# A routed expert layer: from one region per expert to one region per pair of experts

## The chip, the cores and the metric

The kernel runs on one core of a Trainium2 chip. The metric is device time in microseconds of that core. The kernel before took 7589.02 us (median of three runs, 7568.02 to 7589.64). A separate execution, recorded by the hardware profiler, took 6768.39 us; its span from the first to the last instruction is 6766.6 us.

## The reference, cut to what matters

12,500 nodes with 256 features go through four layers, each added to its input: a relational graph convolution, a feed-forward layer on half of the nodes, a graph attention layer, and a mixture of experts. The change touches the mixture, and the end of the attention layer, where its routing is done.

```python
def _L1_ffn_ref(x, Wg, bg, W1, b1, W2, b2):
    B, S, D, E, H, K = (4, 512, 256, 8, 512, 2)
    gate_scores = x @ Wg + bg
    _, idx = jax.lax.top_k(gate_scores, K)
    mask = jax.nn.one_hot(idx, E, dtype=x.dtype).sum(axis=-2)
    xf = x.reshape(-1, Dv)
    mf = mask.reshape(-1, E)
    h = jax.nn.gelu(jnp.einsum('td,edh->teh', xf, W1) + b1[None], approximate=False)
    y = jnp.einsum('teh,ehd->ted', h, W2) + b2[None]
    out = jnp.einsum('ted,te->td', y, mf)
...
x = x + _L1_ffn_ref(_layernorm(x, axis=-1)[None], ...)[0]
```

So every token is multiplied with the weights of exactly two of eight experts, and the two results, their two biases b2 and the token itself are added up without a weight.

## The kernel before, in words

The edges are handled in 1661 tiles of 128. The relational layer and the attention layer each fetch one row per edge by an indirect gather on POOL (`gather`, L234), one instruction per tile, and sum them into nodes with matmuls against a one-hot matrix (L921). In the attention layer (`even_gat`) the order of all work is written out by a small planner: a step is one tile, and each piece of work is put at a step and may yield some steps between its parts. The engines' queues are then held to that order (`tc.manual_schedule`).

When the nodes of two windows of the attention layer are complete, a "quad" of four tiles of 128 nodes goes to `route` (L673). It normalizes the nodes, computes the eight gate scores, and makes a mask `mk` with a one at the two best experts (L697 to L713). Two small matmuls count, for each expert, how many tokens came before (L717, L718); `run` holds the totals. From these each token gets two slot numbers `toI`, one in each of its experts' regions of the DRAM table XS (L720 to L732). Then POOL scatters the normalized row, with its node number as a 257th element, twice: one indirect DMA per tile of 128 tokens and expert choice, eight per quad (L740). They are issued behind the latest gather (`behind`). Last, `route` multiplies the mask with the biases b2, adds the token itself and writes that to the DRAM table O2 (L747 to L760).

`finish` fills the ends of the eight regions with 256 empty slots each by 16 scatters (L774), and works out, for 105 groups of 256 slots, where each begins and which expert it has (`ATD`).

`slots` (L818) is the expert stage. It loads all weights into SBUF (Wall, 8 MB) and runs 105 groups. For each, SP reads the group's row and expert into registers (L848, L850), loads 256 slots (`xs`) and copies one expert's weights from Wall into `we` by a 1 MB DMA. PE transposes the slots, multiplies with W1 (L872), ACT applies gelu (L874), PE multiplies with W2 (L878), DVE copies the result out (L881), and POOL adds it to the rows of O2 by an indirect DMA that accumulates (L882), two per group. Since two experts add to the same row, these scatters are kept in order. At the end O2 is copied to `out` (L886, L889).

Of the kernel before, what the change touches and what calls it, by code (L numbers as in the profile page):

```python
# [30 lines left out]
SP = mybir.EngineType.SP  # L31
ORDERED = {mybir.EngineType.PE, DVE, mybir.EngineType.Activation, SP}
# [68 lines left out]
def gnn_ffn_kernel(ctx: ExitStack, tc: tile.TileContext, x, src, dst, etype, eweight, w_rel, wr, br,  # L101
# [542 lines left out]
    SLOTS = 256  # L644
    REGION = NM * P + SLOTS
    NG = (2 * N + NE * (SLOTS - 1)) // SLOTS
    KE = EH // P
    XS = dram.tile([(NE + 1) * REGION, D + 1], F32, name="XS")
    O2 = dram.tile([N + SLOTS, D], F32, name="O2")
    ATD = dram.tile([2, NG], I32, name="ATD")  # L650

    def router(st):
# [5 lines left out]
        b2s = wp.tile([NE, D], F32, name="b2s")  # L658
        nc.sync.dma_start(b2s, b2)
# [4 lines left out]
        region = wp.tile([P, NE], F32, name="region")  # L664
        nc.gpsimd.iota(region, pattern=[[REGION, NE]], base=0, channel_multiplier=0,
                       allow_small_or_imprecise_dtypes=True)
        run = wp.tile([P, NE], F32, name="run")
        nc.vector.tensor_copy(run, region)
        real = wp.tile([P, 1], F32, name="real")
        nc.vector.tensor_scalar(real, node[:, NM - 1:NM], float(N), None, op0=OP.is_lt)  # L670
        filled = []

        def route(ms, xg, wk, pst, psy, psc, behind=None):  # L673
# [4 lines left out]
            ln_stats(xg, mv[:, :G], wk)  # L678
            yield 3
            xe = wk.tile([P, 4, D + 1], F32, name="xe", bufs=3)  # L680
            nc.vector.tensor_copy(xe[:, :G, D], node[:, ms[0]:ms[0] + G])
            gt = wk.tile([P, 4, NE], F32, name="gt")
            pg = psc[0].tile([P, 4, NE], F32, name=psc[1])
            for i, m in enumerate(ms):
                normalized(xe[:, i, :D], xg[:, i, :], mv[:, i, :])
                yield 1
                pt = pst[0].tile([P, 2, P], F32, name=pst[1])
                for k in range(2):
                    transpose(pt[:, k, :], xe[:, i, k * P:(k + 1) * P])
                yield 1  # L690
                xT = wk.tile([P, 2, P], F32, name="xT")
                evac(xT, pt)
                yield 1
                for k in range(2):
                    nc.tensor.matmul(pg[:, i, :], xT[:, k, :], Wgs[:, k, :], start=k == 0, stop=k == 1)
# [18 lines left out]
            yield 1  # L714

            pp_ = psc[0].tile([P, 2, 4, NE], F32, name=psc[1])
            nc.tensor.matmul(pp_[:, 0, :G, :], before, mk[:, :G, :], start=True, stop=True)  # L717
            nc.tensor.matmul(pp_[:, 1, :G, :], ones, mk[:, :G, :], start=True, stop=True)  # L718
            yield 2
            pos = wk.tile([P, 4, NE], F32, name="pos")  # L720
            for i in range(G):
                nc.vector.tensor_tensor(pos[:, i, :], pp_[:, 0, i, :], run, op=OP.add)
                nc.vector.tensor_tensor(run, pp_[:, 1, i, :], run, op=OP.add)
            yield 1
            far = wk.tile([P, 4, NE], F32, name="far")
            nc.vector.tensor_scalar(far[:, :G, :], mk[:, :G, :], -float(NOWHERE), float(NOWHERE),
                                    op0=OP.mult, op1=OP.add)
            nc.vector.tensor_tensor(far[:, :G, :], far[:, :G, :], pos[:, :G, :], op=OP.add)
            nc.vector.tensor_tensor(pos[:, :G, :], pos[:, :G, :], mk[:, :G, :], op=OP.mult)
            toI = wk.tile([P, 2, 4], I32, name="toI", bufs=3)  # L730
            nc.vector.tensor_reduce(toI[:, 0, :G], far[:, :G, :], axis=AX.X, op=OP.min)
            nc.vector.tensor_reduce(toI[:, 1, :G], pos[:, :G, :], axis=AX.X, op=OP.max)  # L732
            yield 3
            for i, m in enumerate(ms):
                n = rows(m)
                for j in range(2):
                    if i or j:
                        yield 2
                    with tc.issue_after(behind().ins) if behind else nullcontext():
                        ins = nc.gpsimd.indirect_dma_start(  # L740
                            out=XS, out_offset=bass.IndirectOffsetOnAxis(ap=toI[:n, j, i:i + 1], axis=0),
                            in_=xe[:n, i, :], in_offset=None)
                    tc.declare_no_dep(ins.ins, group="slots", reason="each slot is written once")
                    tc.add_to_no_dep_group("slots", ins.ins)
                    filled.append(ins.ins.name)

            o = wk.tile([P, 4, D], F32, name="o")  # L747
            for i, m in enumerate(ms):
                pt = pst[0].tile([P, 2, P], F32, name=pst[1])
                transpose(pt[:NE, 0, :], mk[:, i, :])  # L750
                yield 1
                mT = wk.tile([NE, P], F32, name="mT")
                nc.scalar.activation(mT, pt[:NE, 0, :], AF.Copy)
                yield 1
                pb = psy[0].tile([P, D], F32, name=psy[1])
                nc.tensor.matmul(pb, mT, b2s, start=True, stop=True)
                yield 2
                nc.vector.tensor_tensor(o[:, i, :], pb, xg[:, i, :], op=OP.add)
                n = rows(m)
                nc.sync.dma_start(O2[m * P:m * P + n, :], o[:n, i, :])  # L760

        def finish():

            pad = wp.tile([P, SLOTS // P, D + 1], F32, name="pad")
# [931 lines left out]
```

## Time and profile before

| what | us |
|---|---|
| median of three runs | 7589.02 |
| profiled execution | 6768.39 |
| its span | 6766.6 |
| relational layer and feed-forward, gathers at full rate | about 500 to 2650 |
| attention layer with route | about 3000 to 5400 |
| end of route, padding, loading of the weights | 5400 to 5511 |
| expert stage, to the last scatter's landing | 5511 to 6723 |
| copy of O2 to out | 6723 to 6766.6 |

Over the whole span PE is busy 84%, DVE 43%, ACT 11%, POOL 57%. A busy share says little by itself: PE's clock is granted by a throttle, 0.734 of full speed on average here, and a slow PE looks busy. In a table of stretches each row has the stretch, its length, then busy time and number of instructions of PE, PE's weight loads, DVE, ACT and POOL, the granted clock, the busy share of the DMA engines and GB/s. In a list of groups a row has line, engine, operation, output<-input, shape and count, then busy time and mean ns of one, then the idle time before them and what ended it. "issue" is time in which the engine waited for nothing that the profile shows.

### The profile page before, as it was taken

The page shows a single profiled execution, that of the slowest core. Times are in us where ns is not written, and L with a number is a line of the kernel's source. Part 1 is how long each engine was busy: PE and PEld are TensorE (multiplying, and loading weights), DVE is VectorE, ACT ScalarE, POOL GpSimd, SP SyncE. Part 2 cuts the span into 40 slices and gives each one's busy share as a digit, 9 for nine tenths or more (in the row PEclk, how much of TensorE's full clock was granted, in tenths as well). Part 3 has the DMA queues.
Part 4 walks back from the last instruction along what each step waited for, and adds up shares of the span by engine and source line. Part 5 has one row for each costly group of instructions (what it writes and reads, how often), then busy time and mean ns, then how long its engine had stood idle before and what let it go on. Part 6 is the DMA issues. An engine that isn't in the chain of part 4 may idle for free. (4 is left out here: it accounts for less than half of the span.)

```text
span 6766.6 us, 77763 instructions
## 1 busy us (share of the span) xinstructions
PE 5684.5 (84%) x28042; PEld 4806.8 (71%) x28042; DVE 2938.0 (43%) x7741; ACT 753.3 (11%) x1553; POOL 3886.8 (57%) x3768
## 2 busy tenths in 40 slices
PE   6979999999999998548898899898998947777775
PEld 3447777777777786438888888888887836656664
DVE  6642333333333332766666666666666621111110
ACT  2320000000000001110000000000000011212121
POOL 0017777777777774047777777777777522222222
PEclk9986778777778878775555555555565668888887
DMA  7763333333333332455555555555555345555555
GB/s 244 303 259 107 114 113 109 112 111 114 113 112 114 113 113 75 149 157 139 141 142 142 142 140 145 141 142 142 143 141 138 105 148 140 140 140 133 136 145 153
DMA packets 437378, 949.51 MB, mean 140 GB/s; under 512 B 84371, under 2 KB 293222, under 8 KB 410783
## 3 DMA queue, kind: packets, MB, share of 16 engines
q0 software_dynamic: 199872, 494.39, 28.1%
q1 hardware_dynamic: 237108, 450.03, 21.3%
q8 instruction: 224, 3.67, 0.2%
q14 instruction: 174, 1.42, 0.1%
HBM read 617.71 MB, written 228.88 MB: 125 GB/s over the span
## 5 line engine op out<-in xcount | busy, mean ns | idle before, releaser
L234 POOL DMA_INDIRECT row<-T,rowC x1661 | 1668.3, 1004 | 567.1 <-issue 221.3
L234 POOL DMA_INDIRECT rows<-T1A,srcC x1661 | 1666.1, 1003 | 512.0 <-issue 428.1
L921 PE MATMUL bin<-S,rows 128*128 128x96 f32 (+5 forms) x8756 | 1822.6, 380 | 3.6 <-DVE rows L1269 3.3
L921 PEld LDWEIGHTS bin<-S,rows 128*128 128x128 f32 x8756 | 1739.3, 298 | 79.4 <-issue 67.7
L921 PEld LDWEIGHTS bin<-S,row 128*128 128x128 f32 x7700 | 1281.7, 247 | 333.8 <-DMA row<-T,rowC 206.2
L921 PE MATMUL bin<-S,row 128*128 128x96 f32 (+5 forms) x7700 | 1374.3, 335 | 118.7 <-DMA row<-T,rowC 105.2
L882 POOL DMA_INDIRECT O<-y,toI x210 | 326.9, 1556 | 911.1 <-DVE y L881 420.1
L872 PE MATMUL ph<-xT,we 128*128 128x256 f32 x1680 | 475.3, 446 | 270.7 <-DVE xT L191 265.7
L872 PEld LDWEIGHTS ph<-xT,we 128*128 128x128 f32 x1680 | 376.0, 229 | 349.2 <-DVE xT L191 278.8
L930 DVE TENSOR_TENSOR S<-lcC,col 128x576 f32<-128x576 f32 x554 | 415.4, 750 | 395.5 <-PE bin L921 395.2
L1269 DVE TENSOR_TENSOR rows<-rows,pw 128x1536 f32<-128x1536 f32 x277 | 482.9, 1743 | 30.9 <-PE pw L195 30.8
L861 DVE CAST toI<-xs 128x2 int32<-128x2 f32 x105 | 17.7, 169 | 1024.0 <-DMA O<-y,toI 812.7
L1001 PE MATMUL ph<-xT,w1s 128*128 128x512 f32 (+1 forms) x800 | 411.4, 644 | 1.3 <-DVE xT L191 1.3
L878 PE MATMUL py<-we,hT 128*128 128x256 f32 x1680 | 380.5, 379 | 2.9 <-DVE y L881 2.9
L1009 PE MATMUL pt<-w2s,hT 128*128 128x256 f32 x1568 | 375.4, 383 | 0.0
L469 PE MATMUL pm<-BD,xT 128*128 128x512 f32 x784 | 351.4, 601 | 12.8 <-ACT xT L189 12.3
L878 PEld LDWEIGHTS py<-we,hT 128*128 128x128 f32 x1680 | 319.0, 190 | 47.3 <-DVE y L881 4.1
L189 ACT ACTIVATE xT<-pt 128x256 f32<-128x256 f32 x301 | 115.5, 384 | 1780.4 <-PE pt L195 1548.5
L1009 PEld LDWEIGHTS pt<-w2s,hT 128*128 128x128 f32 x1568 | 283.9, 190 | 31.4 <-PE ph L1001 0.2
L1015 DVE TENSOR_TENSOR y<-pt,b2B 128x256 f32<-128x256 f32 x98 | 41.6, 424 | 571.2 <-PE pt L1009 571.2
L469 PEld LDWEIGHTS pm<-BD,xT 128*128 128x128 f32 x784 | 145.6, 191 | 189.8 <-issue 154.1
L874 ACT ACTIVATE hT<-ph,we 128x256 f32<-128x256 f32 x420 | 199.3, 474 | 674.4 <-PE ph L872 674.4
(266 smaller groups left out, 4885.2 us busy)
## 6 DMA issues: line engine op xcount, KB each, us to landing
we<-Wall SPq DMA_DIRECT2D x105, 1026.0 KB
T<-tb SPq DMA_DIRECT2D x97, 1024.0 KB
dmB<-DMN SPq DMA_DIRECT2D x277, 192.0 KB
xs<-XS SPq DMA_DIRECT2D x105, 257.0 KB
row<-T,rowC POOLq DMA_INDIRECT x1661
rows<-T1A,srcC POOLq DMA_INDIRECT x1661
xg<-in_x_dram SPq DMA_DIRECT2D x48, 512.0 KB
T1A<-t SPq DMA_DIRECT2D x97, 130.0 KB
```

The source lines that it names most:

```text
L189: nc.scalar.activation(dst_ap, src_ap, AF.Copy)
L234: return nc.gpsimd.indirect_dma_start(out=o, out_offset=None, in_=table, in_offset=bass.IndirectOffsetOnAxis(ap=idx, axis=0))
L469: nc.tensor.matmul(pm, xT[:, k, :], BD[:, k, r4:r4 + 4, :], start=True, stop=True)
L872: nc.tensor.matmul(ph, we[:, k * EH + f * P:k * EH + (f + 1) * P], xT[:, k, :], start=k == 0, stop=k == 1)
L874: nc.scalar.activation(hT[:, f, :], ph, AF.Gelu, bias=we[:, A2 + f:A2 + f + 1])
L878: nc.tensor.matmul(py, hT[:, f, i * P:(i + 1) * P], we[:, A1 + f * D:A1 + (f + 1) * D], start=f == 0, stop=f == KE - 1)
L882: nc.gpsimd.indirect_dma_start(out=O2, out_offset=bass.IndirectOffsetOnAxis(ap=toI[:, i:i + 1], axis=0), in_=y, in_offset=None, compute_op ...
L921: nc.tensor.matmul(open_[b][k][:, lo - b * size:hi - b * size], lhs(k), S[:, lo - base:hi - base], start=False, stop=last[b] == t and (siz ...
L930: nc.vector.tensor_tensor(S[:, :n], lcC[:, t:t + n, None].to_broadcast([P, n, WIN]), col[:, None, :WIN].to_broadcast([P, n, WIN]), op=OP.i ...
L1001: nc.tensor.matmul(ph[:, :G * P], w1s[:, k, f * P:(f + 1) * P], xT[:, k, :G * P], start=k == 0, stop=k == 1)
L1009: nc.tensor.matmul(py, hT[:, f, i * P:(i + 1) * P], w2s[:, f, :], start=f == 0, stop=f == KH - 1)
L1269: nc.vector.tensor_tensor(r, r, group[g]["w"][:, o:o + c, :, None].to_broadcast([P, c, H, CH]), op=OP.mult)
```

## The change

Tokens are no longer put into one region per expert but into one region per pair of experts: eight experts make 28 pairs. A token has one slot. Two pairs share one stretch of the table XS, one growing upwards, the other downwards. A slot holds the token itself, not normalized, its node number, and its mean and reciprocal deviation (259 elements).

- `route` multiplies the mask with itself into 64 pair entries per token, counts those, and scatters each token once. Nothing is written to O2; O2 and its initialization are gone.
- `finish` pads the 28 regions by 28 scatters, and works out 128 groups' rows and their two experts. Full groups come first, then the partly filled ones, then empty ones.
- `slots` runs groups of 128 slots, 116 of them always and nine more behind a branch. DVE normalizes the tokens, copies the two experts' W1 from SBUF to SBUF (their numbers read by DVE into registers) and adds the two b2; ACT copies the two W2. PE accumulates both experts' results in one PSUM tile. DVE adds the token, and POOL scatters the rows to `out` without accumulation; empty slots have a node number out of bounds and are not written. The work of five groups in a row is interleaved in an order written by hand: in each step the newest group's load comes first, then the next part of each older group, and the oldest group's product with W2 last.

```diff
-    SLOTS = 256
-    REGION = NM * P + SLOTS
-    NG = (2 * N + NE * (SLOTS - 1)) // SLOTS
+    NP = NE * (NE - 1) // 2
+    REGION = NM * P + 2 * P
+    NG = (N + NP * (P - 1)) // P
+    NFULL = -(-(N - NP * (P - 1)) // P)
+    SURE = min(NG, max(NFULL, -(-N // P) + NP * 2 // 3))
...
+            pair = q1
+            for i in range(G):
+                nc.vector.tensor_tensor(pair[:, i], mk[:, i, :, None].to_broadcast([P, NE, NE]),
+                                        mk[:, i, None, :].to_broadcast([P, NE, NE]), op=OP.mult)
+            nc.vector.tensor_tensor(pair[:, :G], pair[:, :G], lower[:, :G], op=OP.mult)
+            yield 1
+            pp_ = psc[0].tile([P, 2, 4, NE, NE], F32, name=psc[1])
+            nc.tensor.matmul(pp_[:, 0, :G], before, pair[:, :G], start=True, stop=True)
+            nc.tensor.matmul(pp_[:, 1, :G], ones, pair[:, :G], start=True, stop=True)
             yield 2
...
             for i, m in enumerate(ms):
                 n = rows(m)
-                for j in range(2):
-                    if i or j:
-                        yield 2
...
+                if i:
+                    yield 2
+                with tc.issue_after(behind().ins) if behind else nullcontext():
+                    filled.append(to_slots(toI[:n, i:i + 1], xg[:n, i, :]))
-
-            o = wk.tile([P, 4, D], F32, name="o")
-            for i, m in enumerate(ms):
-                pt = pst[0].tile([P, 2, P], F32, name=pst[1])
-                transpose(pt[:NE, 0, :], mk[:, i, :])
...
-                nc.tensor.matmul(pb, mT, b2s, start=True, stop=True)
...
-                nc.sync.dma_start(O2[m * P:m * P + n, :], o[:n, i, :])
...
+            for e in range(NE):
+                for f in range(e):
+                    padded.append(to_slots(padI[:, e, f:f + 1], pad))
...
+            def group(g, begin):
+                row = number(g, 0, SP, ROWS)
+                xs = wk.tile([P, SW], F32, name="xs", bufs=6)
+                load = nc.sync.dma_start(xs, XS[bass.ds(row, P), :])
...
+                yield
+                we, w2 = [], []
+                for j in range(2):
+                    e = number(g, 1 + j, DVE, NE - 1)
+                    we.append(wk.tile([P, A1 + KE], F32, name=f"we{j}"))
+                    nc.vector.tensor_copy(we[j], W1all[:, bass.ds(e, 1), :].rearrange("p o w -> p (o w)"))
+                    if j == 0:
+                        xn = wk.tile([P, D], F32, name="xn")
+                        normalized(xn, xs[:, :D], xs[:, D + 1:])
+                        toI = wk.tile([P, 1], I32, name="toI", bufs=5)
+                        nc.vector.tensor_copy(toI, xs[:, D:D + 1])
+                    xb = xs[:, :D]
+                    nc.vector.tensor_tensor(xb, xb, b2B[:, bass.ds(e, 1), :].rearrange("p o w -> p (o w)"), op=OP.add)
+                yield
+                pt = pst.tile([P, 2, P], F32, name="pt")
+                for k in range(2):
+                    transpose(pt[:, k, :], xn[:, k * P:(k + 1) * P])
+                xT = wk.tile([P, 2, P], F32, name="xT")
+                nc.vector.tensor_copy(xT, pt)
+                yield
+                hT = wk.tile([P, 2, KE, P], F32, name="hT")
+                for j in range(2):
+                    ph = psh.tile([P, KE, P], F32, name="ph")
+                    for f in range(KE):
+                        for k in range(2):
+                            nc.tensor.matmul(ph[:, f, :], we[j][:, k * EH + f * P:k * EH + (f + 1) * P], xT[:, k, :],
+                                             start=k == 0, stop=k == 1)
+                        nc.scalar.activation(hT[:, j, f, :], ph[:, f, :], AF.Gelu, bias=we[j][:, A1 + f:A1 + f + 1])
+                for j in range(2):
+                    e = number(g, 1 + j, ACT, NE - 1)
+                    w2.append(wk.tile([P, KE * D], F32, name=f"w2{j}", bufs=2))
+                    nc.scalar.activation(w2[j], W2all[:, bass.ds(e, 1), :].rearrange("p o w -> p (o w)"), AF.Copy)
+                yield
+                py = psy.tile([P, D], F32, name="py")
+                for j in range(2):
+                    for f in range(KE):
+                        nc.tensor.matmul(py, hT[:, j, f, :], w2[j][:, f * D:(f + 1) * D],
+                                         start=j == 0 and f == 0, stop=j == 1 and f == KE - 1)
+                y = wk.tile([P, D], F32, name="y", bufs=4)
+                nc.vector.tensor_tensor(y, py, xb, op=OP.add)
+                ins = nc.gpsimd.indirect_dma_start(
+                    out=out, out_offset=bass.IndirectOffsetOnAxis(ap=toI, axis=0), in_=y, in_offset=None,
+                    bounds_check=N - 1, oob_is_err=False)
+                tc.declare_no_dep(ins.ins, group="rows", reason="each row is written once")
...
+            def work(lo, hi):
+                with tc.manual_schedule(engines=ORDERED):
+                    parts = []
+                    for s in range(hi - lo + 4):
+                        if lo + s < hi:
+                            parts.append(group(lo + s, s == 0))
+                        for p in parts[::-1]:
+                            next(p, None)
+                        parts = parts[-4:]
+
+            work(0, SURE)
+            if SURE < NG:
+                many = nc.values_load(at[0:1, 0, 3:4], min_val=0, max_val=P)
+                with tc.If(many > SURE):
+                    work(SURE, NG)
```

## The prediction

> **What bounds the kernel now.** I read the stages first (the table of stretches), then the groups of the two stages that the diff touches, then waits and the chain. Columns of a stretch: PE, PEld, DVE, ACT, POOL busy, granted TensorE clock, DMA share, GB/s.
>
> ```profile
> 4400.00:4600.00 200.00, 181.28 (x1015) 171.22 (x1014) 126.28 (x297) 11.69 (x29) 153.36 (x154) 0.59 0.55 142
> ...
> 5800.00:6000.00 200.00, 149.88 (x648) 124.72 (x647) 22.13 (x73) 41.08 (x90) 54.48 (x35) 0.89 0.55 144
> ```
>
> The attention stage (3000 to 5400 us, where route runs too) has 152 to 157 POOL operations in every 200 us: one per 1.30 us, like a metronome. The groups of 3000:5400 say why:
>
> ```profile
> L234 POOL DMA_INDIRECT rows<-T1A,srcC x1633 | 1627.9, 997 | 497.5 <-issue 419.9 <-PE bin L921 27.8 <-DMA rows<-T1A,srcC 10.7
> ...
> L740 POOL DMA_INDIRECT XS<-xe,toI x184 | 184.2, 1001 | 64.2 <-issue 49.1 <-DVE toI L732 8.4 <-DMA XS<-xe,toI 1.5
> ...
> L756 PE MATMUL pt<-b2s,mT 8*128 8x256 f32 x182 | 102.9, 663 | 0.0
> ```
>
> A gather or scatter is 1.00 us plus 0.30 us of issue, back to back; POOL waits for almost nobody. POOL is the bound, although PE looks busier: PE runs at a clock of 0.59 and still keeps up.
>
> The expert stage (5511 to 6723 us) is different: PE 75% busy, clock 0.89, POOL 27%. Its waits (5400:6767) and its chain:
>
> ```profile
> DVE toI L861 <- DMA O<-y,toI: 812.7, 78, 14.7
> ...
> POOL O L882 <- DMA O<-y,toI: 390.3, 97, 7.2
> ```
> ```profile
> DMA 12%; issue 3%; PE 1%; DVE 1%; DVEq 0%; POOLq 0%
> ```
>
> The accumulating scatters into O2 wait for each other (3.7 us to land, then 0.69 us to start the next: 4.4 us each in the chain), 210 of them are 210 x 4.4 = 924 us of the 1212 us; toI waits on them too, and PE stands until it gets xT. So this stage is bound by that chain, at 1206 / 105 = 11.5 us a group. The end of the timeline:
>
> ```profile
> 6719.48 1.55 POOL L882 DMA_INDIRECT O<-y,toI  x1 [2.87 <-DMA O<-y,toI]
> 6723.15 0.62 SPq L886 DMA_DIRECT2D out_dram<-O  x1
> ```
>
> From 6723.1 to 6766.6 the program only copies O2 to out: 43.5 us.
>
> **The change, part by part**, against this execution (6768.4 us; span 6766.6).
>
> 1. Route, one scatter per token: 92 of the 184 scatters in 3000:5400 go, 92 x 1.30 = **-120 us** on POOL. What comes next is PE and DVE. PE loses per quad four mask transposes (0.38 us), four b2 products (1.22 us for two instructions) and gains four 256-column count matmuls instead of 32-column ones (0.61 against 0.30 us each at half clock): -6.4 + 1.2 = -5.2 us, as much as POOL loses (4 x 1.30), so PE's share stays. DVE loses 2.6 us a quad (four o at 0.42, the far and pos steps) and gains about 3.9 (five products, 256-wide pos steps at 0.42): +1.3 x 25 = 33 us on an engine 64% busy: 0. The count matmuls wait for about 1.3 us more of DVE, with the bin matmuls queued behind; 12 buffers of gathered rows cover it. If PE were the bound, the same -5.2 x 24 = -125 comes from PE, or, if the new wait eats it, 0.
> 2. Tail of that stage: two scatters fewer at the end, no o writes, a longer pos chain: **-2**. finish has about 38 small DVE operations at 0.2 us, as long as the twenty old ones (5451 to 5461), under the pads.
> 3. Pads: 28 instead of 16. SP waited 16.3 us for them at L822 before it could load weights, and each is 0.97 + 0.30: 12 x 1.27 = **+15**. If the new pool didn't need their memory: 0.
> 4. Loads: Wall's 8 MB came in 5485 to 5511; b2 broadcast is another 1 MB: **+3**. The first group's way to its first ph (5511 to 5517 before; now a W1 copy, normalize, transpose, xT) is about as long: 0.
> 5. Expert stage, 116 groups always (counting the reference's choices on these inputs gives 113 groups in 28 pairs, so the branch to nine more isn't taken). PE per group: py has 16 instructions of 256 columns, ph 32 of 128 columns, each with its own weights. Rows:
>
> ```profile
> 6005.53 3.62 PE L878 MATMUL py<-we,hT 128*128 128x256 f32 x16
> ...
> 6008.77 0.57 PEld L195 LDWEIGHTS pt<-ident,xs 128*128 128x128 f32 x4
> ...
> 5410.07 4.10 PEld L921 LDWEIGHTS bin<-S,rows 128*128 128x128 f32 x36
> ```
>
> py: 16 x 0.214 = 3.43 us. For ph, half of 0.214 is 0.107; 36 loads in 4.10 us are 0.114 apiece; the transposes take 0.145. I take 0.12, nearest to the loads: 32 x 0.12 = 3.84. Transposes: 0.60. PE: 7.87 us.
>
> Does PE wait? In the hand order a step is, on PE: transposes of group s-2, ph of s-3, py of s-4; on ACT: gelus and then the two W2 copies of s-3; on DVE: W1 copies and normalizing of s-1, xT of s-2, y of s-4. Each input of PE was begun a step earlier. The tightest is py's: the W2 copies stand on ACT behind the gelus, and py of that group comes a whole py, transposes and ph later (7.9 us). ACT: a gelu takes 0.474 us at 256 columns, about 0.37 at 128, x8 = 3.0; a copy 0.384 at 256 and 0.597 at 512 columns, so 1.02 at 1024, x2; two reads of the expert's number into a register: SP's reads of `at` took 0.27 us where DMA was idle and 0.9 to 1.2 where it was full, plus 0.2 of register work; the new stage moves 0.26 MB a group instead of 1.3, so 0.5. ACT 6.0 us, its copies done 3 us after ph. DVE: y 0.42, xT 0.42, normalize 0.41, toI 0.16, two additions 0.84, two reads 1.0, two W1 copies (a 128x1664 cast SBUF to SBUF took 1.03 us, so 0.70 for 1028 columns) 1.4: 4.7 us. y waits for py's end with the next group's W1 copies and xT queued behind it; they are needed a step later, 2.8 us of slack. POOL 1.3 us. The 1 MB DMA for `we` is gone. So PE is the bound, without a pause, at full clock: **T = 7.9 us**, 116 x 7.87 + 5 for the last scatter = 918, against 1206: **-288**. Ends: 0.107 and 0.45 for the transposes give 7.3 us (-354); 0.145 gives 8.7 (-192); DVE with every price at its worst, 9 us (-157).
> 6. out is written by the scatters: -43.5; the branch at the end costs what the branch on sortedness did (18.3 to 22.2 us): **-39**.
>
> Sum: -120 - 2 + 15 + 3 - 288 - 39 = **-431 us**, 6768 to 6337. The median of the runs is 7589, 821 us above the profiled execution, and no view says where. The same difference gives 7158, the same ratio 7106; I say **7150**, nearer to the difference, since PE's clock may be what is slower there, and PE bounds the new stage.
>
> **Two rules against the change.** The clock:
>
> ```profile
> 1012.00:1015.00 3.00, 3.00 (x16) 3.00 (x16) 0.00 (x0) 0.23 (x1) 2.39 (x3) 0.50 0.39 104
> ...
> 6003.00:6006.00 3.00, 3.00 (x16) 2.64 (x15) 0.82 (x3) 1.69 (x4) 1.06 (x1) 1.00 1.00 342
> ...
> 6036.00:6039.00 3.00, 0.00 (x0) 0.00 (x0) 0.00 (x0) 0.00 (x0) 0.00 (x0) 0.90 1.02 302
> ```
>
> The Trainium skill ("TensorE: Matmul & The Clock Gate", Part 1) says that an idle window of about 3.4 us halves the clock. By it a stage without pauses is warm. The rows say less: in 6036 to 6039 the clock falls in a real pause, but at 1012 to 1015 PE was busy all the time and had half its clock, in a row of 80- and 16-column matmuls. Sorting the trace's 3.4 us steps by the share of time that moving columns fill: at full clock 698 of 698 with 0.55 or more kept it, 42 of 47 at 0.5, 23 of 41 at 0.4, 2 of 129 below; from half clock about 0.8 brings it back. ph fills 0.107/0.12 = 0.89, py all: kept, and regained at the start. A hole of 2 us would leave (3.4 - 2) / 3.4 x 0.9 = 0.37 and, where it falls into one step, cost 1.7 us more: by the rule nothing, by the rows up to 116 x 1.7 = 197 us if each group had one. I take the rows, and no hole. The other: "SBUF — State Buffer" (section "Who interferes with whom") says that a DVE copy in a two-port mode keeps POOL from writing descriptors; the 1.03 us for 1664 columns is that mode. Two W1 copies are 1.4 us a group, 162 in all if added. POOL is idle 6.6 of 7.9 us: 0. The other way round, a scatter can hold a W1 copy up for 1 us: DVE 5.7 of 7.9, 0 too. Without that cover y's four buffers run out and PE waits.
>
> **Rivals.**
> - *DVE is the bound of the expert stage*: reads at the loaded price (1.2 + 0.2 each, +1.8), W1 copies at one column per cycle like a 128x1536 tensor_tensor (1.74 us, so 1.2 each, +1.0), held up by POOL (+1): 4.7 + 3.8 = 8.5, with semaphores 9: 116 x 9 + 5 = 1049, -157 there, -300 in all: **7289**. For it: SP's reads had a median of 0.9. Against it: a fifth of the DMA traffic, and the 1.03 us row.
> - *The attention stage gives nothing* (PE late on the count matmuls): -311: **7278**. Against it: POOL's metronome.
> - *Slower*: PE stays at half clock in the expert stage: 32 x 0.24 + 16 x 0.43 + 1.2 = 15.7 us a group, 116 x 15.7 + 5 = 1826, +620 there, +477 in all: **8066**. It decides from T = 7.87 + 431/116 = 11.6, that is a mean clock of 0.68. For it: attention runs at 0.59 with a busy PE, and the unexplained 821 us. Against it: the filled share of 0.89; attention's matmuls are narrow.
> - *Nine more groups run*: excluded by the count.
>
> **Chances.** Likeliest 0.63 (own range 7050 to 7240), DVE 0.15, no gain in attention 0.12, slower 0.10 (of which 0.02 within 0.3%, where the clock lands near the turning point). 0.3% (23 us) is what a measurement here can tell from no change. Faster 0.88, same 0.03, slower 0.09. Range: low 7030 (T = 7.3, -497, taken as a ratio), high 7400 (DVE bound and half of attention's gain gone, -240, and some of the way to the slower one); it leaves out the slower case and the tails.
>
> **What would show it.** POOL 153 operations per 200 us still, but 92 fewer, stage 120 us shorter; in the expert stage PE busy above 95% at a clock near 1.0, 7.9 us a group, ph instructions 0.12 apart, DVE under 6 us a group; the end within 6 us of the last scatter. Wrong if the clock there is below 0.9, if PE waits for DVE or ACT, or if POOL in attention waits for others than issue.

## The result: 2.4 per cent slower, and where the time is

The changed kernel took 7767.2 us in the median of four runs (7751 to 7782), the kernel before 7583.5 (7568 to 7590): a ratio of 1.0244, with an interval of 1.0223 to 1.0264. The forecast was 7150.

Every kernel ran at one of two levels, the unchanged one at 6740 to 6786 us in some sittings and at 7568 to 7653 in others; the first profile of before lies at the lower level and the times beside it at the upper, so what follows compares runs and stages of one level. The changed kernel, run again at the lower level, took 6960.5 against 6753.8 there, 1.0305 (1.0287 to 1.0322). Its loss is 184 us at the upper and 207 us at the lower level, and the traces of the lower level can be laid beside the profile that the prediction worked from:

| stage, in us | before (first profile) | changed | one tile per product | predicted change |
|---|---|---|---|---|
| start to the first row gather | 2953.5 | 2941.8 | 2944.3 | 0 |
| first to last row gather (attention, route) | 2403.0 | 2280.8 | 2279.6 | -120 |
| last gather to the load of `at` (tail, pads) | 128.9 | 139.0 | 140.3 | +13 |
| load of `at` to the end of the span | 1281.2 | 1625.0 | 894.4 | -324 |
| span | 6766.6 | 6986.6 | 6258.6 | -431 |

The column "one tile per product" belongs to an experiment below. The column "changed" says that the route's part came as predicted (-122 and +10), and that the expert stage, with the copy that it replaces, became 344 us longer where 324 less were forecast. (The 9 to 12 us ahead of the first gather were not predicted, and nothing here explains them.)

First the stretches (columns as in the prediction: PE, PEld, DVE, ACT, POOL busy, granted clock, DMA share, GB/s). The changed kernel at the lower level:

```profile
4400.00:4600.00 200.00, 175.32 (x1005) 170.78 (x1004) 137.11 (x320) 9.82 (x21) 153.00 (x155) 0.59 0.52 139
...
6000.00:6200.00 200.00, 160.04 (x732) 129.81 (x730) 49.09 (x120) 72.13 (x147) 15.25 (x15) 0.80 0.07 20
```

In attention POOL issues 155 operations in 200 us, as before: the metronome is still the bound, with fewer operations to issue. Of the scatters, these groups of 3000:5360 are left (the second are the pads):

```profile
L696 POOL DMA_INDIRECT XS<-xg,toI x98 | 100.3, 1023 | 113.3 <-DVE toI L767 74.1 <-issue 26.2 <-DVE part L802 10.2
...
L696 POOL DMA_INDIRECT XS<-pad,padI x28 | 27.2, 971 | 12.4 <-issue 7.9 <-DMA XS<-pad 4.1 <-DMA XS<-pad,padI 0.3
```

In the expert stage nothing is full: PE is at 80 per cent with a clock of 0.80 (0.82 from 5430 to 6950 us), ACT at 36, POOL at 8, DMA at 7. The forecast was PE above 95 per cent at a clock near 1. The waits of that stage, in the changed kernel's measured profile (6200:7700), say who stands for whom:

```profile
ACT hT L911 <- PE ph L909: 913.8, 830, 3.6
PEld ph L909 <- ACT hT L911: 447.9, 665, 0.8
PE ph L909 <- ACT hT L911: 303.9, 665, 0.5
```

The first line alone would be harmless: a gelu waits for its product. The other two are the finding: **PE and its weight loads wait for the gelu**, 665 times in about 110 groups, so six times a group. The timeline shows how (start, duration, operation, and in brackets the idle time before it):

```profile
6508.13 0.71 PE L909 MATMUL ph<-xT,we 128*128 128x128 f32 x4 [0.46 <-ACT hT L911]
6508.88 0.37 ACT L911 ACTIVATE hT<-ph,we 128x128 f32<-128x128 f32 x1 [0.80 <-PE ph L909]
6509.30 0.71 PE L909 MATMUL ph<-xT,we 128*128 128x128 f32 x4 [0.46 <-ACT hT L911]
...
6514.97 3.62 PE L920 MATMUL py<-w,hT 128*128 128x256 f32 x16
...
6518.42 0.38 PE L196 MATMUL pt<-ident,xn 128*128 128x128 f32 x2
...
6525.94 1.22 PE L909 MATMUL ph<-xT,we 128*128 128x128 f32 x4 [0.46 <-ACT hT L911]
6527.19 0.37 ACT L911 ACTIVATE hT<-ph,we 128x128 f32<-128x128 f32 x1 [1.31 <-PE ph L909]
...
6528.63 5.62 PE L920 MATMUL py<-w,hT 128*128 128x256 f32 x16
...
6534.09 0.38 PE L196 MATMUL pt<-ident,xn 128*128 128x128 f32 x2
```

A product (four instructions), its gelu, the next product, its gelu: PE and ACT take turns, 1.17 us a turn (6508.13 to 6509.30). The group from the transposes at 6506.85 to those at 6518.42 takes 11.6 us at full clock. The next one begins warm, loses the clock on its way (products of 1.22 us, py 5.62 instead of 3.62) and takes 15.7. Of 106 groups 50 kept the full clock and 44 took 15.7 us. Over the stage a group takes 13.5 us on the mean; the forecast was 7.9, the old stage's groups 11.5.

The code that does it is in the order of two lines of the diff: `ph = psh.tile([P, KE, P], ...)` stands ahead of the loop over f, so the four products of an expert lie in one PSUM tile, and product f + 1 is not written into it before the gelu of product f has read from it. The old loop took a new tile for each product. At the end no copy follows, as forecast. The span ends 11.8 us after the start of the last scatter, where the prediction had said within 6.

```profile
7736.94 0.42 DVE L923 TENSOR_TENSOR y<-py,xs 128x256 f32<-128x256 f32 x1 [3.03 <-PE py L920]
7737.64 0.98 POOL L924 DMA_INDIRECT out_dram<-y,toI  x1 [2.47 <-DVE y L923]
```

### The profile page after: what moved, and what is told of

Its sections match the earlier page's. It is cut to its first block, busy times and chain, and to the rows that moved or that the text cites. A ratio compares the mean times of both kernels' runs of the same rounds, so it can differ in the third digit from the quotient of the medians.

```text
span 7749.4 us, 83201 instructions
## 1 busy us (share of the span) xinstructions
PE 5907.8 (76%) x29768; PEld 5024.4 (65%) x29768; DVE 3216.3 (42%) x8337; ACT 1063.1 (14%) x2090; POOL 3548.1 (46%) x3587
## 4 chain that ended last, share of the span: by engine, by line
PE 50%; issue 28%; DVE 11%; another core or an unknown queue 6%; POOL 2%; ACT 1%; DMA 1%; DVEq 0%; POOLq 0%; SPq 0%; ACTq 0%
PE bin L976 30%; PE ph L1056 5%; PE pm L470 5%; PE pt L1064 4%; PE pt L196 2%; DVE rows L1323 2%; POOL out_dram L924 1%; PE pt L725 1%; PE py L1128 1%; DVE ln_st L215 1%; DVE S L985 1%; PE px L1285 1%; POOL rows L235 0%; PE bin L966 0%
## 5 line engine op out<-in xcount | busy, mean ns | idle before, releaser
L976 PE MATMUL bin<-S,row 128*128 128x96 f32 (+5 forms) x7700 | 1236.6, 319 | 103.5 <-issue 100.0
L909 PE MATMUL ph<-xT,we 128*128 128x128 f32 x3712 | 746.3, 339 | 323.5 <-ACT hT L911 322.0
L909 PEld LDWEIGHTS ph<-xT,we 128*128 128x128 f32 x3712 | 578.5, 226 | 475.6 <-ACT hT L911 473.7
L924 POOL DMA_INDIRECT out_dram<-y,toI x116 | 115.1, 992 | 1504.5 <-DVE y L923 1419.2
L920 PE MATMUL py<-w,hT 128*128 128x256 f32 x1856 | 525.0, 447 | 0.0
L196 PE MATMUL pt<-ident,xn 128*128 128x128 f32 x1016 | 230.7, 329 | 353.4 <-DVE xn L220 242.2
L911 ACT ACTIVATE hT<-ph,we 128x128 f32<-128x128 f32 x928 | 340.8, 367 | 961.7 <-PE ph L909 957.1
L920 PEld LDWEIGHTS py<-w,hT 128*128 128x128 f32 x1856 | 424.5, 235 | 72.7
L196 PEld LDWEIGHTS pt<-ident,xn 128*128 128x128 f32 x1016 | 152.1, 177 | 420.1 <-issue 293.5
L1056 PEld LDWEIGHTS ph<-xT,w1s 128*128 128x128 f32 x800 | 152.1, 210 | 250.6 <-issue 177.7
```

The costliest lines, as they stand in the source:

```text
L196: nc.tensor.transpose(o, i, ident[:k, :k])
L909: nc.tensor.matmul(ph[:, f, :], we[j][:, k * EH + f * P:k * EH + (f + 1) * P], xT[:, k, :], start=k == 0, stop=k == 1)
L911: nc.scalar.activation(hT[:, j, f, :], ph[:, f, :], AF.Gelu, bias=we[j][:, A1 + f:A1 + f + 1])
L920: nc.tensor.matmul(py, hT[:, j, f, :], w2[j][:, f * D:(f + 1) * D], start=j == 0 and f == 0, stop=j == 1 and f == KE - 1)
L924: ins = nc.gpsimd.indirect_dma_start(out=out, out_offset=bass.IndirectOffsetOnAxis(ap=toI, axis=0), in_=y, in_offset=None, bounds_check=N ...
L976: nc.tensor.matmul(open_[b][k][:, lo - b * size:hi - b * size], lhs(k), S[:, lo - base:hi - base], start=False, stop=last[b] == t and (siz ...
```

## The experiments

**The first profile of before.** The unchanged kernel, profiled once more.

> The kernel before, unchanged, profiled once more. Theory A (the first profile of it, 6768 us, was an odd execution; ordinary executions have pauses of PE and POOL in the two gather stages that no instruction of the kernel causes, as the changed kernel's profile shows them, 138 POOL operations per 200 us instead of 153): this profile has a span near 7570 us, POOL at about 138 per 200 us in the relational stage, and an attention stage of about 2900 us. Theory B (the changed kernel itself brings those pauses): span near 6770 us and 153 operations per 200 us, with the timed run beside it still at 7580.

It took 7619.8 us, with 7629.6 for the runs beside it. The stretch 3600:4600 of the first profile, and of this one:

```profile
3600.00:4600.00 1000.00, 894.89 (x4993) 847.21 (x4992) 641.45 (x1506) 58.38 (x144) 765.90 (x769) 0.59 0.54 142
```

```profile
3600.00:4600.00 1000.00, 754.09 (x3964) 702.24 (x3963) 511.59 (x1209) 46.17 (x114) 603.54 (x612) 0.56 0.42 113
```

The same work, with 612 POOL operations a millisecond instead of 769, a clock of 0.56 instead of 0.59, and less DMA: the stages with gathers take longer (2976 us against 2403 for this one), the expert stage does not (1266 against 1281). What POOL waits for between 3300 and 5300 us at the upper level:

```profile
POOL rows L234 <- issue: 297.4, 963, 4.3
POOL rows L234 <- PE bin L921: 228.1, 67, 16.4
```

Waits of up to 16 us for PE are new. So the 821 us of which the prediction says that "no view says where" are pauses in both gather stages, common to both kernels: the two profiles of before are 851 us apart, 275 of it ahead of the first row gather and 573 from there to the last. What makes the pauses stays open. Fetches of instructions don't coincide with them: of 412 us in which the weight loads stood for over 1.5 us at a time (500 to 3100 us), under 5 us lie at a transfer of one of the two instruction queues.

**A tile for each product.** The suspected wait alone is taken away:

```diff
                 for j in range(2):
-                    ph = psh.tile([P, KE, P], F32, name="ph")
                     for f in range(KE):
+                        ph = psh.tile([P, KE, P], F32, name="ph")
                         for k in range(2):
-                            nc.tensor.matmul(ph[:, f, :], ...)
+                            nc.tensor.matmul(ph[:, 0, :], ...)
...
```

> The changed kernel, but each of the eight W1 products of a group has a PSUM tile of its own (four buffers, one bank each) instead of four products in one tile. Theory A (in the changed kernel PE waits for each gelu before it may write the next quarter of the same tile, 665 waits of 0.46 us in 6200:7700, which also thins PE so that its clock falls): the waits of ph for hT go, a group takes 7.9 to 8.5 us instead of 13.4, the expert stage is about 600 us shorter, and the kernel runs in about 7150 us. Rival (the register reads, the W2 copies or DVE hold PE): the waits move elsewhere, a group stays above 11 us and the time above 7480 us.

7092.8 us (7088 to 7101), 0.9295 of the kernel before (0.9271 to 0.932). It beats both kernels. Its expert stage as stretch, and a group of it in the timeline:

```profile
6600.00:6800.00 200.00, 200.00 (x1379) 187.19 (x1378) 89.99 (x220) 137.29 (x277) 27.00 (x27) 1.00 0.13 38
```

```profile
6605.19 3.74 PE L909 MATMUL ph<-xT,we 128*128 128x128 f32 x32
6605.84 3.50 ACT L911 ACTIVATE hT<-ph,we 128x128 f32<-128x128 f32 x8 [1.44 <-PE ph L909]
6608.76 3.62 PE L920 MATMUL py<-w,hT 128*128 128x256 f32 x16
```

PE is busy all the time at full clock. The 32 instructions of ph run as one row, the eight gelus beside them, and every group takes 7.25 us. The waits of PE for hT are gone from the list.

**How the wait and the clock share the loss.** Four runs at the lower level. The first keeps the shared tile and gives PE more work, in the time in which it stands:

```diff
                         nc.scalar.activation(hT[:, j, f, :], ph[:, f, :], AF.Gelu, ...)
+                        nc.tensor.matmul(fill[:, :2 * P], we[j][:, :P], xT.rearrange("p k n -> p (k n)"),
+                                         start=True, stop=True)
```

> Edit: the changed kernel, its shared ph tile kept, with one more matmul after each product (128 weights, 256 columns of xT, into a PSUM tile of its own that nobody reads): more work for PE, put into the time in which it waits for the gelu. In the changed kernel's trace a group takes 11.6 us when its matmuls are at full clock and 15.7 when they are not, 13.6 on the mean. Theory A (the wait costs 11.6 - 7.25 = 4.4 us a group, and another 2.0 because a PE that stands 0.46 us of every 1.17 loses its clock): the filler, 0.43 us a product at full clock, fits into the 0.46 us wait and holds the clock, so groups take 11.6 to 12.0 us, clock in the stage above 0.97, total 7767 - 116 x 1.6 to 2.0 = 7535 to 7580. Rival B (the clock falls for another reason than the unfilled time): the clock stays near 0.81 and the filler, twice as long in the cold half, comes on top: 7767 + 116 x 1.7 (half of the groups, 8 x 0.43) = 7970 or more.

6858.6 us, 1.0137 of before (1.0108 to 1.0165), against 6960.5 for the changed kernel in a later sitting of this level (before: 6770.0 and 6753.8). Its stretch, and one turn of its timeline:

```profile
6200.00:6400.00 200.00, 197.76 (x1061) 150.22 (x1060) 52.35 (x128) 79.70 (x161) 16.24 (x16) 1.00 0.08 22
```

```profile
6005.37 0.71 PE L911 MATMUL ph<-xT,we 128*128 128x128 f32 x4
6005.92 0.60 PE L914 MATMUL fill<-xT,we 128*128 128x256 f32 x2
6006.12 0.37 ACT L913 ACTIVATE hT<-ph,we 128x128 f32<-128x128 f32 x1 [0.80 <-PE ph L911]
```

The clock is 1.00 throughout, and all groups take 12.45 us. With 3.4 us more matmuls in each group it is some 100 us faster. The expectation's 11.6 to 12.0 forgot that the fourth product of each expert is followed by no wait: two fillers of 0.43 us stick out, and 11.6 + 0.86 is 12.46.

The second takes a new tile for every two products:

```diff
-                    ph = psh.tile([P, KE, P], F32, name="ph")
                     for f in range(KE):
+                        if f % 2 == 0:
+                            ph = psh.tile([P, KE, P], F32, name="ph")
...
```

> Edit: the changed kernel with a new ph tile for every two products instead of every four: four waits for a gelu in a group instead of eight. Theory A (each wait costs (11.6 - 7.25)/8 = 0.54 us at full clock): T = 7.25 + 4 x 0.54 = 9.4 us, PE filled about three quarters of the time, so full clock kept: 7093 + 116 x 2.17 = 7345. If the clock falls in the same share of groups: 9.4 + 2.0 = 11.4, 7575. Rival B (the wait comes from having too few tiles, not from sharing one): with twice as many tiles in use and still four buffers no better than the changed kernel, 7767.

6602.5 us, 0.9752 of before (0.9725 to 0.9779); all groups 10.14 us, at full clock. The list of waits (5500:6580):

```profile
PEld ph L910 <- ACT hT L912: 276.1, 426, 0.7
PE ph L910 <- ACT hT L912: 195.0, 426, 0.5
```

426 waits in 107 groups are four a group, as expected. The price of one was mis-sized: I had divided by eight waits in the changed kernel, but the first product into a fresh tile has nothing to wait for, so there are six, and (11.58 - 7.25)/6 = 0.72 us each; 7.25 + 4 x 0.72 is 10.13. A wait costs more than the 0.46 us that its line shows: a turn takes 1.17 us, a product's four instructions back to back 0.45. The rest is in the product itself, whose row of four takes 0.71 us when it stands alone.

The third asks what the wait follows, the tile or the bank of PSUM that it lies in:

```diff
-            psh = mo.enter_context(tc.tile_pool(name="ms_ph", bufs=4, space=PSUM))
+            psh = mo.enter_context(tc.tile_pool(name="ms_ph", bufs=1, space=PSUM))
...
-                    ph = psh.tile([P, KE, P], F32, name="ph")
+                    ph = psh.tile([P, KE, 4 * P], F32, name="ph")
...
```

> Edit: the changed kernel with one ph tile for all experts, four PSUM banks wide, product f in bank f of it. Tells apart what the wait of the changed kernel follows. If it follows the bank (or the bytes): product f waits for the gelu of four products earlier, long done, as in the run with a tile for each product: 7.25 to 7.4 us a group, 7090 to 7120. If it follows the tile's name: every product waits for the gelu before it, 13.6 us a group, 7767.

7033.7 us in one execution, groups of 13.85 us on the mean (12.3 the fastest). Between 5500 and 7000 us:

```profile
PE ph L909 <- ACT hT L911: 347.0, 759, 0.5
```

Seven waits a group, though each product has a bank to itself: the wait follows the tile. (The profile finds a releaser by its semaphore, so this is a wait that was built into the program, tile by tile.) The seventh is the second expert's first product, which now meets the first expert's tile, and 7.25 + 7 x 0.72 = 12.3 is the fastest group. Taking another piece of the same tile doesn't help; another tile does. That the pieces were moved to banks of their own doesn't release them here, but within one bank the wait could not be left out either: the Trainium skill ("PSUM — Partial Sum Buffer", section "PSUM bank collisions raise a hardware error") has two engines kept out of one bank of the same partitions at the same time, whatever columns they touch. No run here tries that.

The fourth is about the route. It takes the version with a tile for each product and puts one scatter per token back:

```diff
                 with tc.issue_after(behind().ins) if behind else nullcontext():
                     filled.append(to_slots(toI[:n, i:i + 1], xg[:n, i, :]))
+                yield 2
+                with tc.issue_after(behind().ins) if behind else nullcontext():
+                    to_slots(toI[:n, i:i + 1], xg[:n, i, :], XS2)
```

> Edit: the version with a tile for each product, with route's second scatter of each token put back (its rows go to a DRAM tensor that nobody reads), everything else of the new route kept. That version's attention stage took 2814 us from first to last row gather and the unchanged kernel's 2976 beside it: 162 less, where the prediction said 120. Theory A (POOL sets the pace, 1.30 us for each of the 97 scatters that come back): +120 to +130 us, 7215 to 7222. Rival B (the gain came from elsewhere in route: the b2 products, the mask transposes and the o rows that PE, DVE and the queue of SP no longer handle): +0 to +40, 7093 to 7135. If the scatter has more than its POOL time behind it (in the pauses that this stage shows): +160 to +210, 7255 to 7300.

6372.0 us. From the first to the last row gather it took 2395.7 us, and 2279.6 in the same kernel without these scatters, run later at the same level. Of the 98 scatters that came back 88 lie in this stretch (176 instead of 88), so 116 us are 1.32 us each, where the prediction had 1.30. In time, 6372.0 against 6254.9 is 117: the other ten, behind the last gather, cost nothing that shows. The b2 products, mask transposes and row writes that the change also took out are worth 7 us at most here, since the unchanged kernel, with as many scatters, took 2403.0.

```profile
3600.00:4600.00 1000.00, 831.43 (x4838) 805.96 (x4838) 646.15 (x1516) 48.62 (x103) 766.33 (x768) 0.60 0.52 136
```

```profile
3600.00:4600.00 1000.00, 872.85 (x5173) 847.83 (x5172) 696.02 (x1645) 51.27 (x109) 766.14 (x768) 0.61 0.52 139
```

768 POOL operations a millisecond with the scatters (first row) and without them (second). Theory A holds here. At the upper level the stage became 162 to 210 us shorter; that this contains its pauses is likely and not shown.

**The same at one level, and the old stage's bound.** The changed kernel and the version with a tile for each product side by side:

> The changed kernel once more, beside the version with a tile for each product and the unchanged kernel on one chip. The runs so far come from two chips: one on which the unchanged kernel takes 7580 to 7630 us and the row gathers' stage shows pauses, and one on which it takes 6770, as in the first profile. Theory A (what the changed kernel loses is all in the expert stage, 13.6 us a group whatever the chip): on the slow chip 1.024 times the unchanged kernel; on the fast chip -124 in attention, +10 between, +374 behind, -39 at the end counted in it: about 6990, 1.03 times. Rival B (the chip is what made the difference): on the fast chip below 6770.

> The version with a ph tile for each product again, in the same call as the changed kernel. Theory A: the whole difference to the changed kernel is 116 x (13.55 - 7.25) = 731 us less 12 at the start of the stage or more, so 0.90 to 0.91 of it on any chip: about 7093 on the slow chip, 6250 to 6260 on the fast one (the run with the second scatter put back took 6372 there, and its attention stage 117 longer than that of its neighbours). The prediction's sum for a stage without pauses was 6337 from 6768.

6960.5 us (1.0305 of before) and 6254.9 (6254 to 6260; 0.9261, 0.9245 to 0.9276). Both are near what was expected; the table above is theirs. Then the old kernel, with its chain of accumulating scatters split in two (what O3 gathers is not added to the output):

```diff
                     nc.gpsimd.indirect_dma_start(
-                        out=O2, out_offset=...
+                        out=(O2, O3)[i % 2], out_offset=...
```

> Edit: the unchanged kernel with its accumulating scatters going by turns into two tensors, O2 and a new O3, so that a scatter waits for the one before the last; O3 gets the residual rows as well, and its sums are left out of the output. Theory A (the chain of scatters into O2 sets the old stage's 11.5 us a group): the chain falls to half, 4.4 us a group, and PE is the next bound, 75% busy of 11.5 us now, 8.6 us a group: 105 x 2.9 = 300 us less from the load of the group table to the end, perhaps 10 to 20 more in attention for the 97 more row writes: total -280 (6490 on the fast chip, 7310 on the slow one). Rival B (PE, or the 1 MB weights of each group, already set it): within 30 us of the unchanged kernel.

6417.9 us, 0.9502 (0.9486 to 0.9518). The stage from the load of the group table to the end of its last engine's work is 886 us instead of 1236; a group takes 8.1 us on the mean instead of 11.5.

```profile
6000.00:6200.00 200.00, 187.71 (x888) 160.32 (x887) 29.85 (x96) 56.06 (x123) 77.00 (x50) 1.00 0.73 195
```

PE at 94 per cent and full clock, where the old kernel had 75 per cent and 0.89. So the prediction's reading of what bound the old stage is right. (The gain is 336 us where 280 were expected: the expectation left PE its old clock, and that rose from 0.87 to 1.00.) It also puts the new stage into its place: with a tile for each product it takes 884.5 us up to the same point. The gain of the expert stage is that of loosening the chain of sums; the pairing is one way to do it. (Adding O3 to the output, which this kernel leaves out, would cost time that was not measured.)

**How little work holds the clock.** The shared tile again, with fillers only where a wait follows, of 256, 128 and 64 columns:

```diff
+                        if f < KE - 1:
+                            nc.tensor.matmul(fill[:, :64], we[j][:, :P], xT.rearrange("p k n -> p (k n)")[:, :64],
+                                             start=True, stop=True)
```

> Edit: the changed kernel, one ph tile for four products, with the filler matmul of 256 columns only after the products that a wait for a gelu follows (three of four). In the run with a filler after every product a group took 12.45 us, which is 11.6 + 2 x 0.43 for the two fillers that no wait hides. Theory A (the waits cost 4.35 us a group at full clock, the lost clock 1.95): with these two fillers gone 11.6 us a group, clock 1.00, 116 x 1.93 = 224 us less than the changed kernel: 6736 where the unchanged kernel takes 6754, so as fast as the unchanged one (7535 to 7545 where it takes 7580 to 7630). Columns fill (0.43 + 0.43)/1.17 = 0.73 of the time between two products. Rival B (the clock follows real pauses of some 3 us, as the rule has it): the changed kernel would not have lost it in pauses of 0.46 us.

> Edit: the same with a filler of 128 columns: columns fill (0.43 + 0.21)/1.17 = 0.55 of the time between two products, the share that kept the clock in every step of the first trace. If that reading is the rule: clock 1.00 and 11.6 us a group, the same time as with 256 columns within 15 us. If half of the time is not enough: groups of 15 us among those of 11.6, as in the changed kernel, up to 224 us more.

> Edit: the same with a filler of 64 columns: columns fill (0.43 + 0.11)/1.17 = 0.46 of the time between two products, against 0.37 in the changed kernel, which alternates between warm and cold groups. By the first trace's steps (42 of 47 kept the clock at a share of 0.5, 23 of 41 at 0.4) some groups lose it: mean 11.8 to 13 us, clock 0.85 to 0.98, 30 to 160 us above the run with 256 columns. If the time is 11.6 already, the border lies between 0.37 and 0.46; if 13.5, above 0.46.

6761.8 us with 256 columns (0.9996 of before, 0.9982 to 1.001), 6755.4 with 128 and 6764.6 with 64, in one execution each. The stretches of the three:

```profile
6000.00:6200.00 200.00, 197.54 (x1074) 147.88 (x1073) 57.56 (x142) 84.77 (x172) 18.22 (x18) 1.00 0.08 25
```

```profile
6000.00:6200.00 200.00, 175.61 (x1074) 147.94 (x1074) 55.93 (x137) 85.21 (x173) 17.25 (x17) 1.00 0.08 23
```

```profile
6000.00:6200.00 200.00, 170.10 (x1071) 147.89 (x1071) 55.59 (x136) 85.13 (x173) 17.18 (x17) 1.00 0.08 23
```

All three hold a clock of 1.00, and all groups take 11.58 us, with 64 columns too, where the expectation had some groups lose the clock. So the changed kernel's 13.53 us are 7.25 of work, 4.33 of waits and 1.95 of lost clock: 116 x 4.33 = 502 us and 116 x 1.95 = 226 us, 728 together. The two profiled spans of the table are 728.0 us apart. The medians of the same two kernels are 705.6 apart, which leaves about 203 us for the clock. With the waits and the full clock the kernel is as fast as before: the waits eat up the change's gain, and the lost clock is what makes it slower.

## Why the prediction was wrong

- **What bounds the kernel now**: right in both stages. POOL sets attention's pace (the scatter put back costs 116 us), the chain of sums set the old expert stage's (split, -336 us).
- **Parts 1 to 3**, route, tail and pads: -120, -2 and +15 were said, -122 and +10 measured. Of the stage's gain the scatters are 116 us. Parts that were costed at nothing, the pair products on DVE and the count matmuls, cost nothing that shows.
- **Part 4 and the start of the stage**: +3 and 0 were said. From the load of `at` to the first py it is 49.2 us with a tile for each product, and 38.3 before: +11. Small, and mis-sized.
- **Part 5, "Does PE wait?"**: this is the step that failed. It went through PE's inputs, found each "begun a step earlier", and concluded "PE is the bound, without a pause". An instruction also waits for the place that it writes to. The four products share a tile whose reader is ACT, so each product but the first of an expert waits for a gelu of its own group and step: six waits of 0.72 us. The rule of the Trainium skill's page on PSUM, named above, should have been weighed here and was not. The diff showed the shared tile (it is made outside the loop over f, where the old code made it inside). An estimate from the prediction's own sizes would have been 7.87 us and six gelus of 0.37 on PE's way, 10.1 us a group, before the hand-overs between the engines and before the clock. With the hand-overs it is 11.58, with the lost clock 13.53.
- **Part 5, the sizes** hold once the wait is gone: 7.25 us a group against 7.87. From ph's first instruction to py's first it is 3.57 us (6605.19 to 6608.76), 0.112 for each of 32, where 0.12 was taken and 0.107 was the lower end. The 0.62 us less are 72 us in 116 groups. Register reads aside, ACT was busy for 5.0 us a group (137.29 of 200 us), as said, and DVE for 3.3 where 3.7 was said; a register read took 0.27 to 0.30 us, where 0.5 was taken with the work around it.
- **Part 6**: -39 was said. From the last engine's work to the end of the span it is 45.6 us before, 9.9 with a tile for each product: -36.
- **The clock rule**: the price was there ("up to 116 x 1.7 = 197 us if each group had one"), and the rows were taken before the rule, as they should be; then no hole was seen. That 197 lies near the measured 203 to 226 is luck: it was worked out for one hole of 2 us a group, and there were six waits of 0.46.
- **The port**: two W1 copies of 0.70 us a group beside a POOL that is busy for 1.0 of 7.25 us cost nothing that shows, as said.
- **The rivals**: the slower one was the right kind, with the wrong cause. Its turning point was 11.6 us a group; at 11.58 us (the fillers) the kernel measures 0.9996 of before. It had PE at half clock all through, because attention's clock was 0.59, and got one chance in ten; a wait of PE for ACT was named only under what would make the prediction wrong. DVE as the bound fell (45 per cent busy with a tile for each product), no gain in attention fell (-122), and 116 groups ran.
- **The level**: with the wait taken out the time at the level of the median was 7092.8, where 7150 was said, and 6254.9 at that of the profile, where the sum gave 6337. The choice of the difference over the ratio mattered little. The reason given for it, that PE's clock is what is slower at the upper level and that PE bounds the new stage, doesn't hold: the old expert stage took 1266 us there and 1281 at the lower.

## What to carry to other kernels

When asking whether an engine waits, go through what each instruction reads and through what it writes: for every tile, who reads it last, and when is it written again. A tile that several matmuls fill piece by piece, with another engine reading each piece, is a chain between two engines, whatever the number of buffers, and here it followed the tile even when the pieces had a bank each. And where short waits thin out PE, count its clock in: here the lost clock cost 0.40 to 0.45 of what the waits themselves did.

## What was not expected of the hardware

- PE lost its clock in pauses far shorter than 3.4 us. PE never stood longer than 0.5 us in a row in the expert stage and still ran half of the groups partly at half clock (mean 0.82). What the runs go by is how full the time is: with columns moving for (4 x 0.107)/1.17 = 0.37 of a turn the clock was lost again and again, with 0.46 (a filler of 64 columns) it was held in every group. Pairs of products with the same wait of 0.46 us between them (0.86/1.62 = 0.53) held it too, so it isn't the length of the pause alone.
- The clock of a trace changes in steps of 3.41 us, and the changed kernel's steps (5430 to 6950 us, lower level) show the border, by the share of each that columns fill (at 0.107 us for 128 columns, twice that at half clock): from full clock, 214 of 214 with 0.40 or more kept it, 11 of 30 from 0.36 to 0.40, none of 39 below. From half clock it came back only after a share of 0.72 or more, which cold products with waits seldom reach. With the fillers of 64 columns no step lay under 0.44. Below 0.40 the share is not all of it: with one tile over four banks 94 of 150 steps under 0.38 kept the clock. The 0.55 that the prediction read from the first trace was thus higher than need be in this stage. A filler adds instructions and weight loads as well as columns, and no run here separates these. The Trainium skill ("TensorE: Matmul & The Clock Gate", Part 1) halves the clock after an idle window of about 3.4 us; as a second way to lose it, it names frequent short idles of PE, which agrees with these runs, and gives no figure for them.
- More matmuls made a kernel faster: six fillers of 256 columns are 2.6 us on PE's 7.25 a group, and the kernel takes 199 us less (6960.5 to 6761.8, in sittings with 6753.8 and 6766.6 for the kernel before). Six of 64 columns did the same in one execution (6764.6).
- The same programs have two levels, 851 us apart in the two profiles of before, 848 of it in the stages that gather by indirect DMA. The expectations speak of two chips, but the runs on the chip numbered 0 lie at either level (7619.8 us for the unchanged kernel in one sitting, 6753.8 in another), so if a number is one chip, the level is not the chip's. What makes it no run here tells.
